# A two-layer pre-activation block on one core: other PReLU paths, statistics in bank ends, another softmax, and a new order

## The chip, the core and the metric

The kernel runs on one core of a Trainium2 chip. The metric is the device time of one execution in microseconds. The core has a matrix engine (TensorE, PE in the profile, its weight loads PEld), a vector engine (VectorE, DVE), an activation engine (ScalarE, ACT), GpSimd (POOL) and SyncE (SP), which here only starts transfers. Matrix products land in PSUM: eight banks of 512 fp32 words in each of 128 partitions. Everything else works on SBUF.

## What is computed

Input x is 16 images of 256 channels, 56 x 56, fp32. Two residual layers follow each other, each on the group-normalised x (32 groups of 8 channels):

```python
def _L0_conv_ref(x, bias, w, cb, move1, alpha, move2, gamma, beta):
    xq = sign(x + bias)
    out = 0
    for i, d in enumerate((1, 3, 5)):               # three dilations, 3x3, 4 channel groups
        y = conv(xq, _bin_weight(w[i]), padding=d, rhs_dilation=d, groups=4)
        y = y + cb[i] - move1[i]
        y = where(y >= 0, y, alpha[i] * y) + move2[i]    # PReLU
        out = out + y
    out = (out - mean_over_channels) * rsqrt(var_over_channels + 1e-5)
    return out * gamma + beta

def _L1_conv_ref(x, ...):                           # 8 heads of 8 channels, 3x3 window
    q, k_in, v_in = 1x1 convolutions of x           # 64 channels each
    k = unfold3x3(k_in) + depthwise3x3(k_in) + biases    # 9 of 8 channels per pixel and head
    v = unfold3x3(v_in) + depthwise3x3(v_in) + biases
    attn = softmax((q * k).sum(channels), over the nine)
    return proj((attn * v).sum(nine))

x = x + _L0_conv_ref(gn(x), ...)
x = x + _L1_conv_ref(gn(x), ...)
```

`_bin_weight` is the sign of the centred weights times their mean absolute value.

## The kernel before

**Tiling.** The 64 channels of a group (NG = 4 groups) lie in partitions twice: the upper half of the image in 64 partitions, the lower half in the other 64. A unit u (two an image) is a strip of 14 rows of each half, cut in two pieces of 7 rows, SN = 392 pixels; a tile of one group and unit is 128 x 2 x 392, written 128x784 in the profile. One pair of PSUM banks holds one such tile, and there are four pairs.

**Stages of an image b.** `signs` loads x by group (xh), takes sums and squares on ScalarE (L643), makes the normalisation's shift in small steps (`group_stats`, `shifts`, 4 columns wide) and writes the signs in bf16 to `sgn` (L667), after which two small transfers copy the halo rows (L679, L680). `conv` multiplies for each unit, group and dilation d: 36 products (9 taps, 4 quadrants of the array) into one pair of banks (L716), and then applies the PReLU. It is split as alpha*y + (1-alpha)*relu(y): for d=0 ScalarE writes alpha*y to the tile ct (L735), for d=1 VectorE adds it to ct (L745), for d=2 ScalarE writes it to a second tile rl (L742); then ScalarE does the relu in place in PSUM (L750), and VectorE adds its share (L755). For d=2 GpSimd adds rl to ct (L761). `channel_norm` squares ct (L799), sums over channels with small products (`lanes_sum`, L769), computes mean and root in steps of 196 columns (L813 to L821), spreads them back over the channels (`lanes_spread`, L783), subtracts the mean (L827), scales (L837), adds to x (L850 on GpSimd) and squares again for the second normalisation (L854). `fold` turns these sums into scaled weights wf (L874) and a bias (L884, L894). `qkv` makes q, k and v (L906, evicted by ScalarE at L924). `scores` makes nine products q*k shifted (L959, mostly on GpSimd), sums them with TensorE (L980, ten terms into one pair of banks) and takes the softmax: transpose, maximum, subtraction, exponentials, sum, reciprocal, product, transpose (L1009 to L1031). The ninth exponential is that of the implied zero-shift term and is kept apart, in the columns behind the scores. `attend` multiplies the weights for ten terms (L1044), VectorE multiplies by v shifted (L1055), GpSimd adds up (L1070), VectorE closes (L1075), and the projection (L1087, L1097) adds to x; four transfers store a unit (L1107).

**The order.** Nothing in this program loops on the chip: every instruction is emitted once, in an order written out by hand or by a program ahead of time. The table `ORDER` gives each operation of each stage a place; image b adds b times `PERIOD`. Keys with ^ hold for the first image, with $ for the last. `Plan.emit` walks the places in order and emits the first operation whose inputs are there and whose buffers are free, so the engines' queues interleave several images' stages: the convolutions of image b+1 stand beside the attention of image b. `ON_VECTOR` names the operations, mostly GpSimd's, that are given to VectorE instead. Each engine takes its own instructions strictly in that order, and semaphores hold an instruction until what it reads is there and what it overwrites has been read. In this framework two instructions that touch the same bank of one PSUM tensor are also ordered.

Buffers are counted: four pairs of banks ("ps"), eight ct, one rl, seven p (products q*k), four m (products with v), four xt (x of a unit).

**Start.** GpSimd clears four sgn tiles and the padded q, k and v tiles (L537); `vectors` (L1115 to L1126) makes per-channel constants on VectorE; six pairs of weight blocks are centred, their signs taken, and transposed by TensorE, and VectorE keeps scales and weights (L1222 to L1224).

Of the kernel before, what the change touches and what calls it, by code (L numbers as in the profile page):

```python
# [34 lines left out]
LANES = 32  # L35
SCALE = (C // NH) ** -0.5
# [36 lines left out]
class Op:  # L73
    def __init__(self, place, emit, bufs):
# [6 lines left out]
PERIOD = 1231  # L81
ORDER = {
    "conv0": (
        -682, -410, -359, -2832, -303, -327, -265, -333, -280, -264, -245, -1566, -289, -213, -969, -970,
        -319, -128, -2067, -24, -3260, -58, -18, -16, -1028, -3936, 5, 17, 18, 101, 198, -321, 208, -3768,
        197, 207, 182, -601, -3937, 20, -15, -19, -199, 30, -146, 111, -2560, 21, -394, -20, -152, -3331,
    ),
    "conv0$": (
        -685, -409, -2692, -2836, -277, -2837, -419, -253, 194, -189, 109, -866, -1791, -207, -131, -440,
        -4781, -30, -3248, 99, -154, -250, -557, -386, -2111, -2366, 32, -462, -149, -2080, 175, -1794,  # L90
        -2185, -2439, 121, 140, -6017, -1732, -220, -9, -641, 100, -155, 112, -1493, 147, -1733, 191, 240,
        149, -865, -2379,
    ),
    "conv0^": (
        -2099, -6338, -223, -5746, -1337, -3215, -66, -5779, -1241, -202, -65, -5786, -1673, 42, -67, -667,
        -358, 124, 92, 358, -3217, 123, 231, 234, -3216, 565, 167, 400, 401, -1668, 228, 318, 504, -54, 229,
        -13, 515, -1726, -288, 227, 402, -115, -71, 40, -72, 517, -1182, 702, -116, -769, -2031, 119,
    ),
    "conv1": (
        160, -122, -123, 185, 199, -740, 209, -834, 265, -287, 150, -2506, -1087, 320, 171, 170, -823, 333,  # L100
        -2428, 361, -1220, 326, -175, 180, -1339, 356, 319, 255, 254, -2493, 355, -1340, 394, -1221, 714,
        746, 632, -113, -2040, 412, -162, -296, -1322, 470, -3611, 514, -1195, 925, -1683, -2369, 905, -1995,
    ),
    "conv1$": (
        56, -644, -645, -1492, 306, -11476, -498, -11477, 418, 239, 237, -3613, 188, 148, 146, 190, -1497,
        248, -878, 152, -867, 292, 151, -2181, -2390, -2392, 192, 98, 66, -864, 773, -432, 813, -1612, 662,
        456, 455, -1613, -818, 419, -28, -29, 44, 774, -431, 816, -434, 953, 968, 284, 678, -660,
    ),
    "conv1^": (
        666, 513, 523, -1198, 726, -697, -757, 826, 776, 581, 725, 830, 871, 682, 522, 601, -2033, 828, 824,  # L110
        695, 832, 829, 724, 578, 835, 715, 711, 612, 609, -2032, 865, 831, 878, 811, 949, 902, 901, 1044,
        1106, 38, 717, 718, 827, 869, 815, 890, -2027, 922, -1136, -964, 940, 959,
    ),
    "first^": (-3247,),
    "fold": (
        1404, -2035, -892, -2087, -3779, -4755, -952, -4221, -7223, -9967, -564, -942, -953, 1414, -949,
        -562, 1455, 407,
    ),
    "fold$": (
        1238, 1089, 753, 927, 1174, 593, 772, 1298, 934, 929, 595, 268, 1484, 297, 648, 1286, 559, -6518,  # L120
    ),
    "fold^": (
        1395, -941, -2847, -582, -784, 793, 792, -861, -863, -1498, -846, 1074, 1037, 696, 1424, -847, 1481,
        1444,
    ),
    "load0": (310,),
    "load0$": (539,),
    "load0^": (744,),
    "load1": (771,),
    "load1$": (614,),  # L130
    "load1^": (-117,),
    "mean0": (
        301, -2124, -1860, -2389, 172,
    ),
    "mean0$": (
        336, 87, 139, -232, -216,
    ),
    "mean0^": (
        785, 930, 214, -4431, 979,
    ),  # L140
    "mean1": (
        719, 911, 1038, -307, 787,
# [218 lines left out]
    "scale0^": (10,),  # L361
    "scale1$": (4,),
    "scale1^": (4,),
    "value0^": (4,),
}


# [1051 lines left out]
```

## Time and profile before

| | us |
|---|---|
| median of 3 runs | 1867.02 |
| lowest and highest | 1861.42, 1869.45 |
| the profiled execution | 1872.31 |
| its span, first to last instruction | 1870.5 |
| its mean granted TensorE clock | 0.979 of full |

| engine | busy us | share of the span |
|---|---|---|
| PE | 1653.7 | 88% |
| VectorE | 1570.8 | 84% |
| GpSimd | 1408.7 | 75% |
| ScalarE | 1314.6 | 70% |

The transfers keep their engines busy for 51.8% of the span. How to read the lines below: a group names the line, engine and operation, then what is written and read with shapes, the count, the busy time and the mean of one, and behind the last bar the idle time of the engine just ahead of these instructions, with what ended it. A line of waits names who waited for whom, for how many us in total, how often, and the longest. A window gives the busy time of PE, PEld, DVE, ACT and POOL in a stretch, each with its count, then the granted clock, the share of the transfer engines and GB/s. Busy times of PE are modelled: an engine that is busy all the time need not run at its full pace.

### The profile page before, as it was taken

The page shows a single profiled execution, that of the slowest core. Times are in us where ns is not written, and L with a number is a line of the kernel's source. Part 1 is how long each engine was busy: PE and PEld are TensorE (multiplying, and loading weights), DVE is VectorE, ACT ScalarE, POOL GpSimd, SP SyncE. Part 2 cuts the span into 40 slices and gives each one's busy share as a digit, 9 for nine tenths or more (in the row PEclk, how much of TensorE's full clock was granted, in tenths as well). Part 3 has the DMA queues.
Part 4 walks back from the last instruction along what each step waited for, and adds up shares of the span by engine and source line. Part 5 has one row for each costly group of instructions (what it writes and reads, how often), then busy time and mean ns, then how long its engine had stood idle before and what let it go on. Part 6 is the DMA issues. An engine that isn't in the chain of part 4 may idle for free.

```text
span 1870.5 us, 62125 instructions
## 1 busy us (share of the span) xinstructions
PE 1653.7 (88%) x27322; PEld 953.1 (51%) x27322; DVE 1570.8 (84%) x2217; ACT 1314.6 (70%) x1861; POOL 1408.7 (75%) x782
## 2 busy tenths in 40 slices
PE   4879899898999989898998989899898989989784
PEld 3546455454545545454554545455454545745341
DVE  8777979979797997979799797979979797997966
ACT  5988778677777867677786777778677787755320
POOL 2147769688686968868696886869688686967865
PEclk9799999999999999999999999999999999999897
DMA  7852655547475554647555464755547467223023
GB/s 178 200 113 43 143 123 122 126 93 155 96 158 111 124 126 92 149 102 155 115 120 124 96 151 101 156 113 124 123 94 150 101 147 172 62 69 74 11 61 69
DMA packets 102094, 217.03 MB, mean 116 GB/s; under 512 B 10816, under 2 KB 84672, under 8 KB 101568
## 3 DMA queue, kind: packets, MB, share of 16 engines
q1 hardware_dynamic: 101824, 213.06, 51.8%
q8 instruction: 214, 3.51, 0.8%
q14 instruction: 56, 0.46, 0.1%
HBM read 156.23 MB, written 51.38 MB: 111 GB/s over the span
## 4 chain that ended last, share of the span: by engine, by line
PE 53%; POOL 18%; DVE 16%; issue 6%; ACT 4%; DMA 1%; SPq 0%; POOLq 0%; DVEq 0%; ACTq 0%
PE banks L716 19%; POOL m L1070 13%; PE banks L906 12%; PE banks L980 9%; DVE m L1055 4%; PE banks L1044 3%; PE banks L769 3%; POOL xt L850 3%; PE banks L1087 2%; ACT banks L750 2%; DVE rl L755 2%; DVE ct L755 2%; POOL p L959 1%; POOL ct L761 1%; DVE m L1075 1%
## 5 line engine op out<-in xcount | busy, mean ns | idle before, releaser
L716 PE MATMUL banks<-sgn,wconv 64*64 64x392 bf16 x13824 | 656.7, 335 | 60.3 <-DVE m L1055 25.8
L716 PEld LDWEIGHTS <-wconv 64*64 64x64 bf16 x13824 | 442.8, 106 | 279.1 <-issue 94.7
L1070 POOL TENSOR_TENSOR m<-m 128x784 f32<-128x784 f32 x255 | 475.3, 1864 | 95.9 <-DVE m L1055 82.2
L959 POOL TENSOR_TENSOR p<-qt,kt 128x784 f32<-128x784 f32 x267 | 468.1, 1789 | 93.2 <-ACT qt L924 88.0
L750 ACT ACTIVATE banks<-banks,cbi,csc 128x784 f32<-128x784 f32 x384 | 370.3, 973 | 95.8 <-DVE ct L745 95.8
L761 POOL TENSOR_TENSOR ct<-ct,rl 128x784 f32<-128x784 f32 x125 | 233.3, 1866 | 252.7 <-DVE ct L755 147.8
L1044 PE MATMUL banks<-at,wv 64*64 64x392 f32 x2560 | 276.1, 510 | 56.5 <-DVE lv L821 22.6
L1055 DVE SCALAR_TENSOR_TENSOR m<-banks,vb,vt 128x784 f32<-128x784 f32 x288 | 289.6, 1022 | 25.4 <-POOL m L1070 17.6
L755 DVE SCALAR_TENSOR_TENSOR ct<-banks,oalpha,ct 128x784 f32<-128x784 f32 x256 | 258.1, 1026 | 17.1 <-ACT banks L750 16.4
L906 PE MATMUL banks<-xt,wf 64*64 64x392 f32 x3072 | 269.0, 491 | 0.0
L850 POOL TENSOR_TENSOR xt<-xt,ct 128x784 f32<-128x784 f32 x124 | 229.2, 1871 | 1.4 <-DVE ct L837 1.3
L980 PE MATMUL banks<-p,wk 64*64 64x392 f32 x2304 | 213.7, 489 | 2.8 <-POOL p L959 2.6
L742 ACT ACTIVATE rl<-banks,asc 128x784 f32<-128x784 f32 x128 | 116.7, 912 | 107.0 <-PE banks L716 103.0
L906 PEld LDWEIGHTS banks<-xt,wf 64*64 64x64 f32 x3072 | 131.2, 133 | 101.2 <-issue 68.3
L643 ACT ACTIVATE xh<-xh 128x1568 f32<-128x1568 f32 x120 | 180.6, 1507 | 0.7
L735 ACT ACTIVATE ct<-banks,mv,asc 128x784 f32<-128x784 f32 x128 | 128.5, 1004 | 73.0 <-PE banks L716 72.8
L755 DVE SCALAR_TENSOR_TENSOR rl<-banks,oalpha,rl 128x784 f32<-128x784 f32 x128 | 131.8, 1030 | 53.6 <-ACT banks L750 48.8
L1044 PEld LDWEIGHTS banks<-at,wv 64*64 64x64 f32 x2560 | 86.8, 134 | 176.3 <-issue 69.2
L745 DVE SCALAR_TENSOR_TENSOR ct<-banks,asc,ct 128x784 f32<-128x784 f32 x128 | 131.0, 1024 | 24.9 <-PE banks L716 21.3
L980 PEld LDWEIGHTS banks<-p,wk 64*64 64x64 f32 x2304 | 93.1, 133 | 93.4 <-issue 76.2
L854 ACT ACTIVATE ct<-xt,pr 128x784 f32<-128x784 f32 x128 | 120.2, 940 | 25.4 <-POOL xt L850 23.0
L1087 PE MATMUL banks<-m,wp 64*64 64x392 f32 x1024 | 106.4, 518 | 32.1 <-DVE m L1075 29.6
(115 smaller groups left out, 1870.6 us busy)
## 6 DMA issues: line engine op xcount, KB each, us to landing
xh<-in_x SPq DMA_DIRECT2D x248, 392.0 KB, 5.7
xt<-in_x SPq DMA_DIRECT2D x128, 392.0 KB, 9.2
out<-xt SPq DMA_DIRECT2D x128, 392.0 KB, 5.9
sgn<-sgn SPq DMA_DIRECT2D x128, 41.2 KB, 7.6
p<-in_w SPq DMA_DIRECT2D x12, 144.0 KB, 3.2
xt<-in_wk_parts SPq DMA_DIRECT2D x1, 1344.0 KB, 8.1
xt<-in_wv_parts SPq DMA_DIRECT2D x1, 1280.0 KB, 9.4
wq<-in_wqkv SPq DMA_DIRECT2D x1, 384.0 KB, 9.7
```

Source lines behind the costliest of these rows:

```text
L643: lambda func=func, col=col: nc.scalar.activation(inside(g) if b == 0 else image(xh), image(xh), func, accum_out=sums[:, col : col + 1]),
L716: nc.tensor.matmul(out=ps[q * GC : (q + 1) * GC, h, 0:SN], lhsT=wconv[h * GC : (h + 1) * GC, g, d, tap, :], rhs=sgn[g][h * GC : (h + 1) * ...
L750: lambda: nc.scalar.activation(n(), n(), AF.Relu, bias=cbi[:, g, s], scale=csc[:, g, s]),
L755: lambda: nc.vector.scalar_tensor_tensor(to.tile, n(), oalpha[:, g, s], to.tile, ALU.mult, ALU.add),
L761: lambda e: e.tensor_tensor(ct.tile, ct.tile, to.tile, ALU.add),
L850: lambda e, g=g: e.tensor_tensor(xt[:, g], xt[:, g], ct[g].tile, ALU.add),
L906: nc.tensor.matmul(out=ps[h * D : (h + 1) * D, q, 0:SN], lhsT=wf[q * GC : (q + 1) * GC, g, j, :], rhs=xt[q * GC : (q + 1) * GC, g, h, :], ...
L959: e.tensor_tensor(p.tile.rearrange("p x (r w) -> p x r w", w=W), _view(qt[:, 0, u * SN :], [(NU * SN + LANES, 2), (W, SR), (1, W)]), shift ...
L980: nc.tensor.matmul(out=ps[q * D : (q + 1) * D, h, 0:n], lhsT=wk[r, j, :], rhs=rhs, start=s == 0, stop=s == 9,)
L1044: nc.tensor.matmul(out=ps[h * D : (h + 1) * D, q, 0:SN], lhsT=wv[q * D : (q + 1) * D, j, :], rhs=at[q * D : (q + 1) * D, h, 0:SN], start=True,
L1055: lambda j=j, m=m, ps=ps: nc.vector.scalar_tensor_tensor(m.tile.rearrange("p x (r w) -> p x r w", w=W), _view(ps[:, 0, :], [(512, 2), (W, ...
L1070: lambda e, m=m, acc=acc: e.tensor_tensor(acc.tile, acc.tile, m.tile, ALU.add),
```

## The change

- **PReLU.** For d=0 and d=2 the relu is the first step and goes to SBUF: ScalarE writes a scaled relu to ct or rl, and VectorE adds alpha*y from PSUM to it, in one pass each. So that one form serves all signs of 1-alpha, the scale's size goes into the relu (rsc, cbi) and its sign (sgd) is brought in later: for d=2 by a ScalarE pass rl to rl, which also adds the bias mv2; for ct in the sums over channels (weights cms) and in the mean's subtraction. d=1 keeps its three passes. There are two rl buffers.
- **Bank ends.** PSUM becomes one tensor of eight banks; the four pairs are views of it. The small statistics and the bias of `fold` get a buffer kind of their own, "few": the columns from 470 of the odd bank of a pair.
- **Small steps.** In `group_stats`, `channel_norm` and `fold` a square, a copy, a clamp and another copy go from VectorE to ScalarE; the signs in the root's last steps are rearranged (ngam in place of gam).
- **Softmax.** The nine exponentials lie side by side in a tile e9 (104 x 9); one sum takes all nine, and the product with the reciprocal is done by GpSimd (by VectorE in the last image).
- **Clearing.** GpSimd clears one sgn tile and VectorE three; q, k and v are cleared by GpSimd behind the constants. Half of the weights' copies go to ScalarE.
- **Places.** PERIOD becomes 1214, and ORDER and ON_VECTOR are new throughout. VectorE takes one product q*k less in each middle image.

```diff
-PERIOD = 1231
+PERIOD = 1214
 ORDER = {
...
 ON_VECTOR = {
-    "conv0$": (12,),
-    "conv1$": (25, 51),
-    "prod0": (5,),
-    "prod0$": (3, 4, 6, 8),
...
+    "prod0$": (2, 4, 6, 8),
+    "prod1$": (3,),
...
+    "soft0$": (8,),
+    "soft1$": (8,),
 }
...
-    kinds = {"ps": (banks, 4)}
+    kinds = {
+        "ps": [banks[:, 2 * i : 2 * i + 2] for i in range(4)],
+        "few": [banks[:, 2 * i + 1 : 2 * i + 2, TAIL:512] for i in range(4)],
+    }
...
-    kind("rl", UNIT, 1)
+    kind("rl", UNIT, 2)
...
-    for t in (*sgn, *qts, *kts, *vts):
-        nc.gpsimd.memset(t, 0.0)
+    for g, t in enumerate(sgn):
+        (nc.vector if g else nc.gpsimd).memset(t, 0.0)
...
-        dve(lambda: nc.vector.tensor_copy(e[:, 0:n], at(0)), [gp], [e])
-        dve(lambda: tt(m2[:, 0:n], at(0), e[:, 0:n], ALU.mult), [gp, e], [m2])
+        act(lambda: nc.scalar.activation(m2[:, 0:n], at(0), AF.Square), [gp], [m2])
+        act(lambda: nc.scalar.copy(e[:, 0:n], at(0)), [gp], [e])
...
+        stt = nc.vector.scalar_tensor_tensor
+        if d == 1:
             dve(
-                lambda: nc.vector.scalar_tensor_tensor(ct.tile, n(), asc[:, g, s], ct.tile, ALU.mult, ALU.add),
+                lambda: stt(ct.tile, n(), asc[:, g, s], ct.tile, ALU.mult, ALU.add),
                 [ps, ("scales", g, d)],
                 [ct],
             )
         act(
-            lambda: nc.scalar.activation(n(), n(), AF.Relu, bias=cbi[:, g, s], scale=csc[:, g, s]),
-            [("scales", g, d)],
-            [ps],
+            lambda: nc.scalar.activation(
+                n() if d == 1 else to.tile, n(), AF.Relu, bias=cbi[:, g, s], scale=rsc[:, g, s]
+            ),
...
+        if d == 1:
+            dve(lambda: stt(ct.tile, n(), oalpha[:, g, s], ct.tile, ALU.mult, ALU.add), [ps], [ct])
+        else:
+            dve(
+                lambda: stt(to.tile, n(), asc[:, g, s], to.tile, ALU.mult, ALU.add),
+                [ps, ("scales", g, d)],
+                [to],
+            )
+        if d == 2:
+            act(
+                lambda: nc.scalar.activation(
+                    to.tile, to.tile, AF.Identity, bias=mv2[:, g : g + 1], scale=sgd[:, g, 2:3]
+                ),
...
-        dve(lambda: tt(t.tile, mean(), ms.tile, ALU.mult), [ps, ms], [t])
+        act(lambda: nc.scalar.activation(t.tile, mean(), AF.Square), [ps], [t])
...
-        dve(lambda: nc.vector.tensor_scalar(mean(), mean(), 0.0, EPS_LN, ALU.max, ALU.add), [], [ps])
+        act(lambda: nc.scalar.activation(mean(), mean(), AF.Relu), [], [ps])
...
-                lambda g=g: nc.vector.tensor_tensor(ct[g].tile, ct[g].tile, mb[:, :, 0:SN], ALU.subtract),
+                lambda g=g: stt(
+                    ct[g].tile, ct[g].tile, sgd[:, g, 0:1], mb[:, :, 0:SN], ALU.mult, ALU.subtract
+                ),
...
+        dve(lambda: nc.vector.tensor_reduce(sm.tile, ex.tile, AX.X, ALU.add), [(ex, 0), (ex, 1)], [sm])
+        dve(lambda: nc.vector.reciprocal(sm.tile, sm.tile), [], [sm])
+        either(
+            lambda e: e.tensor_tensor(
+                ex[:, :, 0:CH], ex[:, :, 0:CH], sm.tile.unsqueeze(2).broadcast_to([P, NBK, CH]), ALU.mult
+            ),
...
+    def clear():
+        for t in (*qts, *kts, *vts):
+            nc.gpsimd.memset(t, 0.0)
+
+    pool(clear, ["identb"], ["border"])
```

Some lines of the changed program that the prediction names: L725 are the convolution's products, L596 those of `group_stats`, L608 to L616 its steps, L671 the last step of `shifts`, L886 the copy of r, L890 and L909 the last vector steps of `fold` and L899 its products, L1044 the softmax's product, L1080 and L1095 the products with v and their sums, L1112 the projection's products.

## The prediction

> **What bounds the kernel now.** I read the busy table first, then the stages, because four engines between 70% and 88% say that no single one bounds the whole.
>
> ```profile
> PE 1653.7 (88%) x27322; PEld 953.1 (51%) x27322; DVE 1570.8 (84%) x2217; ACT 1314.6 (70%) x1861; POOL 1408.7 (75%) x782
> ```
>
> The starts of L871, once an image, are 149.4 us for image 0, then 259.3, 368.1, 476.9 and so on to 1779.2: the steady period is 109 us. The head is 149 us, the tail behind the last fold 91 us. The windows over one period, cut in halves, and the head and tail (busy us of PE, PEld, DVE, ACT, POOL; then clock and DMA):
>
> ```profile
> 0.00:149.40 149.40, 99.44 (x1814) 67.40 (x1818) 117.86 (x217) 114.12 (x147) 45.78 (x28) 0.91 0.70 160
> 694.85:749.38 54.53, 54.53 (x910) 31.11 (x904) 40.61 (x62) 43.94 (x64) 43.13 (x25) 1.00 0.48 108
> 749.38:803.91 54.53, 45.74 (x764) 26.03 (x760) 52.44 (x68) 37.30 (x51) 45.05 (x25) 0.97 0.62 136
> 694.85:803.91 109.06, 100.27 (x1666) 57.15 (x1660) 93.05 (x128) 81.23 (x114) 88.18 (x49) 0.98 0.55 122
> 1779.20:1870.50 91.30, 62.63 (x656) 26.87 (x648) 56.66 (x58) 10.66 (x20) 54.15 (x28) 0.84 0.27 62
> ```
>
> In the first half PE never rests and DVE has 14 us to spare; in the second DVE works 52.4 of 54.5 us and PE idles 9. An image is bounded in turn by PE and by DVE. The waits and the chain of one period say the same, with one warning: in the second half the chain runs for 20 us through POOL's additions (L1070), so POOL is nearly as late there as DVE.
>
> ```profile
> PE banks L716 <- DVE m L1055: 25.8, 26, 1.1
> ...
> PE banks L716 <- DVE ct L837: 15.9, 14, 1.5
> ```
>
> ```profile
> 779.73 1.87 POOL m L1070
> 781.68 1.85 POOL m L1070
> 783.59 1.87 POOL m L1070
> 785.54 1.87 POOL m L1070
> 787.48 1.86 POOL m L1070
> ```
>
> PE at full pace: 72 to 108 convolution products follow each other at 43 ns, the fp32 ones at 84.5 ns (halves of one instruction), the sums and spreads at 42. With the counts of an image that is 864 x 0.043 + 192 x 0.0845 (qkv) + 160 x 0.085 (scores) + 160 x 0.0845 (values) + 64 x 0.0845 (projection) + 192 x 0.042 + about 2.1 of small ones = 96.1 us. To find what comes on top I lay the rows' durations on the built order: DVE's instructions, less the 7% by which its rows overlap (row means sum to 100.6 us an image, busy is 93.1), against PE's. The stretch in which DVE exceeds PE most runs from 46.9 to 85.2 us of PE's work, with 13.8 us of excess. 96.1 + 13.8 = 109.9, and 109.1 is measured. This sum, made of rows, carries the forecast.
>
> **The change, part by part**, per image. The groups of that one period (busy us, mean ns of one), and one line of the timeline of the start:
>
> ```profile
> L1070 POOL TENSOR_TENSOR m<-m 128x784 f32<-128x784 f32 x16 | 29.7, 1856 | 6.1 <-DVE m L1055 5.3
> ...
> L735 ACT ACTIVATE ct<-banks,mv,asc 128x784 f32<-128x784 f32 x8 | 8.0, 1003 | 3.7 <-PE banks L716 3.7
> ...
> L742 ACT ACTIVATE rl<-banks,asc 128x784 f32<-128x784 f32 x8 | 7.3, 912 | 7.4 <-PE banks L716 7.4
> ...
> L1027 DVE TENSOR_TENSOR et<-et,banks 128x832 f32<-128x832 f32 x2 | 2.0, 1012 | 0.0
> ...
> L816 DVE TENSOR_SCALAR banks<-banks 128x196 f32<-128x196 f32 x2 | 0.7, 370 | 0.1
> ...
> L814 DVE TENSOR_TENSOR lv<-banks,lv 128x196 f32<-128x196 f32 x2 | 0.7, 351 | 0.0
> ```
>
> ```profile
> 3.78 6.94 DVE L1118 TENSOR_SCALAR oalpha<-pr 128x12 f32<-128x12 f32 x1
> ```
>
> *PReLU.* For d=0, ACT's L735 goes (8 x 1.003 = 8.0 us); for d=2, L742 goes (8 x 0.912 = 7.3) and an Identity from rl to rl comes. No row has that source; between L799 (0.851, no pointer operands) and L735 (1.003, two) I take 1.0, so 8.0 back. Relu now writes SBUF: 16 x 0.03 = 0.5. ACT loses 7.3 us, but it is not the bound (81 of 109), so that is worth nothing by itself. What counts is that a pair of banks is held for one ACT pass and one DVE pass instead of two and one: about 0.95 us less, 16 times an image. DVE's work here is unchanged, and the second rl buffer frees DVE of waiting for POOL's addition (L755 rl waits only 0.5 us for POOL now: nothing).
>
> *DVE's small steps to ACT.* L814 and L816 (1.44 us), L599 and L600 twice and L871 (0.8) leave DVE; ACT gets some 2.3 us. In the stage of the root two Vector/Scalar handoffs fall away (L817 waited 3.8 us an image for L816).
>
> *Softmax.* The product leaves DVE (2 x 1.012) and the addition of the ninth (2 x 0.266); the sum runs over 936 instead of 832 elements (+0.26). POOL gets two products. No POOL row has runs of 8 or a broadcast; L1070 scaled to 832 elements gives 1.98 us, the high end is double (4.0), the low end L959's rate (1.9). I take 1.98, the nearest row. The Trainium skill, GPSIMD Engine Reference, section 4.1 (Engine selection), speaks against this step: two-input elementwise work belongs on VectorE, GpSimd being about twice slower. The rows agree on the ratio (1.98 against 1.01), and by that rule alone the move costs 32 x 0.97 = 31 us of chain. By the stage it doesn't: in the after order the chain from scores to values has 9 and 14 us of other PE work laid over it, and DVE is the engine that runs out there. I go by the stage.
>
> *Places.* One product of nine that DVE did in 14 middle images goes back to POOL (DVE -1.25, POOL +1.79). The mean's subtraction becomes the three-operand form: 8 x 0.064 = +0.5 on DVE.
>
> Sum for DVE: -2.03 -0.53 -1.44 -0.80 -1.25 +0.26 +0.51 = -5.3, so 93.0 becomes 87.8. POOL: 88.2 + 1.8 + 4.0 = 94.0. ACT: 81.2 -7.3 +2.3 +0.2 = about 76.5. PE: unchanged.
>
> *Bank ends.* The small statistics no longer take a pair of the four; they sit in the last columns of a bank that a pair also uses. In the built order they are then serialised with that pair's other users. The rule behind it is in the Trainium skill, PSUM — Partial Sum Buffer, section "PSUM bank collisions raise a hardware error": two engines must not touch one bank and quadrant at once, at whatever columns. No row of before shows such a wait. The after order has four or five an image in which PE's next product stands directly behind a small step: L725 behind L611 twice, L1112 behind L890 and L909, L899 behind L1080. Each needs two ACT steps of 0.2, two DVE steps of 0.16 and whatever large DVE row is in front (1.0), against 0 to 1.8 us of PE work laid between: 0 to 2.5 us each. Bounds are 0 and 6 us an image (below zero is not excluded: before, the same statistics took one pair of four out of use for ten steps). I take 2.3. Behind the waiting matmul stand convolution and projection products, and for those DVE waits.
>
> *Stretch by stretch.* The same sum on the after order gives 9.4 us as DVE's largest excess (57.2 to 76.6 us of PE's work) in place of 13.8: less work, and more evenly laid. Period 96.1 + 9.4 + 2.3 - 0.8 (by which the sum overshot before) = 107.0, against 109.1: -2.1 us. Over 15 periods -32.
>
> *Head.* POOL's clearing keeps DVE from its first vectors until 10.7 us (the row of L1118). One sgn stays on POOL (2.2 us), three go to DVE as 1254 words each (at POOL's own pace of 1740 words in 1.6 us, 3.5 us), while DVE waits for its first load (3.7 us) anyway; q, k and v (4.6 us of POOL) are cleared behind identb. Some 18 short vector instructions (about 0.1 each) come, and six casts of 0.75 us go to ACT, which is the busiest engine of the head (114 of 149). Net -4 to +4; I take -3. *Tail:* in the last image DVE keeps four products of the first strip, makes one of the second instead of two, and keeps both softmax products; I take 0. SP issues the same 653 transfers; stores and halo copies come in another order, but DMA is at 0.55 of its engines in the period, so nothing.
>
> The profiled execution took 1872.3 us (span 1870.5), 0.3% above the median of 1867.0. 1872.3 - 35 = 1837, on the scale of the median 1832.
>
> **The rivals.**
>
> *A. The statistics' waits are hidden* (they fall where PE waits for DVE anyway). For it: the four lie just behind the stretch in which DVE is late. Then the period is 96.1 + 9.4 - 0.8 = 104.7, -4.4 us: 1867 - 66 - 3 = about 1798.
>
> *B. POOL becomes the bound, and it is slower.* POOL is idle 20.9 us of a period now, 5.5 for q, 10.6 for ct, 5.3 for m. With 94.0 us of work the period is 94.0 plus what remains of that idle time: it decides against the change as soon as more than 15 us remain, and with all of it the period is 115, 1867 + 15 x 6 = about 1955. With products of 4.0 us the limit falls to 11. For it: the chain of the second half already runs through L1070, and in the after order POOL exceeds PE by 12.4 us over one long stretch (15 to 77). Against it: before, POOL exceeds PE by 13.4 in a shorter one, and PE never rested there, so p's seven buffers and the loose places took that up. As a likely size: 18 us idle, 112, 1910.
>
> *C. What is gained is given back*: the stalls are 4 us or more, the period stays within 0.5 us, 1860 to 1874.
>
> **How the numbers follow.** Expected path (1810 to 1855) 0.5; A 0.22; C 0.13; B 0.15. About 0.5% (9 us) is what a measurement of this kernel can tell from no change. The expected path and A are faster, with a little of the expected path's upper end going into "same": faster 0.74, same 0.11, slower 0.15. Range: from A (1795) up into B's lower part (1885).
>
> **What would show it.** Right: L871's successor (L886) every 107 us; DVE about 88 us busy of it and POOL 94; L1044 on POOL at 2.0 us; idle time of PE in front of L725 and L1112 released by L611, L608 and L890, 2 us an image. Wrong: PE idle behind POOL's p, or DVE m waiting for POOL's L1095 by more than the 17.6 us of now; L1044 on POOL at 3 us or more; a period above 109; a head longer than 149 us.

## The result and the profile after

The changed kernel takes 2005.21 us (median of four runs, 2004.01 to 2014.17), against 1867.95 for the kernel before on the same chip: 1.075 times as long, with an interval of [1.0725, 1.0775]. Its profiled execution has a span of 2003.8 us at a mean granted clock of 0.937 (before 1870.5 and 0.979). I had predicted 1832, between 1795 and 1885.

The busy table of the changed kernel:

```profile
PE 1718.5 (86%) x27322; PEld 1011.3 (50%) x27322; DVE 1491.1 (74%) x1998; ACT 1260.8 (63%) x1889; POOL 1474.5 (74%) x829
...
PEclk9888989899899989989999998999899898999987
```

VectorE has 80 us less to do, ScalarE 54 less and GpSimd 66 more, roughly what the change was expected to do. PE, with the same 27322 instructions, is busy for 65 us longer, and it is idle for 285 us (2003.8 - 1718.5) instead of 217. The whole 133 us by which the span grew are these two: 65 of slower products and 68 of idle time.

The 15 steady periods before, then those of the changed kernel with its head and tail, in windows (busy us of PE, PEld, DVE, ACT, POOL, then the clock):

```profile
149.40:1779.20 1629.80, 1491.66 (x24864) 858.86 (x24856) 1396.23 (x1944) 1189.86 (x1694) 1308.82 (x727) 0.99 0.53 115
```

```profile
163.60:1913.10 1749.50, 1555.33 (x24857) 915.27 (x24860) 1328.46 (x1732) 1130.52 (x1699) 1375.39 (x774) 0.95 0.48 107
0.00:163.62 163.62, 101.50 (x1821) 70.55 (x1822) 106.33 (x215) 119.34 (x171) 42.65 (x27) 0.89 0.65 151
1913.11:2003.80 90.69, 61.71 (x648) 25.48 (x640) 56.29 (x52) 10.96 (x21) 56.46 (x29) 0.86 0.24 54
```

The starts of the fold (L886) give a head of 163.6 us (before 149.4), 15 periods of 116.6 (before 108.65, from 149.4 to 1779.2), and a tail of 90.7 (before 91.3). So 120 us were lost in the periods and 14 in the head. In a period VectorE works 88.6 us in the mean (93.1 before), GpSimd 91.7 (87.3) and ScalarE 75.4 (79.3): none of them is the bound, yet the period is longer. PE works 103.7 us of it and idles for 12.9; before it was 99.4 and 9.2.

Groups of one period, from 756.66 to 877.12 us (busy us, mean ns of one, then the idle time in front and what ended it), and behind them VectorE's last PReLU step (L755) in the period of before that the prediction reads:

```profile
L1095 POOL TENSOR_TENSOR m<-m 128x784 f32<-128x784 f32 x16 | 29.8, 1861 | 15.9 <-DVE m L1080 13.5 <-DVE g L614 1.9
...
L766 ACT ACTIVATE rl<-rl,mv,sgd 128x784 f32<-128x784 f32 x8 | 8.3, 1033 | 2.3 <-DVE rl L760 2.3
...
L757 DVE SCALAR_TENSOR_TENSOR ct<-banks,oalpha,ct 128x784 f32<-128x784 f32 x8 | 8.1, 1026 | 5.0 <-ACT banks L750 5.0
L760 DVE SCALAR_TENSOR_TENSOR ct<-banks,asc,ct 128x784 f32<-128x784 f32 x8 | 8.1, 1020 | 10.1 <-ACT ct L750 10.1
...
L1044 POOL TENSOR_TENSOR e<-e,mx 128x832 f32<-128x832 f32 x2 | 3.3, 1659 | 0.0
```

```profile
L755 DVE SCALAR_TENSOR_TENSOR ct<-banks,oalpha,ct 128x784 f32<-128x784 f32 x16 | 16.1, 1026 | 0.3 <-ACT banks L750 0.3
L755 DVE SCALAR_TENSOR_TENSOR rl<-banks,oalpha,rl 128x784 f32<-128x784 f32 x8 | 8.2, 1030 | 4.7 <-ACT banks L750 4.6
```

VectorE, short of time before, now idles 15 us of this period in front of two of its PReLU steps until ScalarE's relu is there (5 before), and GpSimd idles 13.5 us in front of its additions until VectorE's m is there (5.3 before): the time that was freed became waiting.

One-microsecond windows show how PE loses pace. The pause that ends at 868.85 is 3.6 us long; behind it the clock is 0.50 until about 872, and 16 and 18 products are counted in a us in place of 31:

```profile
866.00:867.00 1.00, 0.00 (x0) 0.00 (x0) 1.00 (x2) 0.35 (x3) 0.40 (x1) 1.00 0.00 0
867.00:868.00 1.00, 0.00 (x0) 0.00 (x0) 1.00 (x2) 0.00 (x0) 0.00 (x0) 1.00 0.00 0
868.00:869.00 1.00, 0.15 (x4) 0.14 (x7) 0.70 (x5) 0.00 (x0) 0.72 (x1) 0.93 0.00 0
869.00:870.00 1.00, 1.00 (x16) 0.72 (x15) 0.00 (x0) 0.00 (x0) 1.00 (x1) 0.50 0.00 0
871.00:872.00 1.00, 1.00 (x18) 0.82 (x12) 0.00 (x0) 0.00 (x0) 0.00 (x0) 0.50 0.00 0
873.00:874.00 1.00, 1.00 (x31) 0.82 (x24) 0.91 (x1) 0.05 (x1) 0.00 (x0) 1.00 0.00 0
```

The chain of waits says what PE waited for there (start, duration, engine and line): two large VectorE steps, then the fold's small ones, then 35 products at 90 ns each, where full pace is 43.

```profile
866.19 1.01 DVE ct L760
867.20 0.94 DVE m L1080
868.14 0.08 DVE g L614
...
868.64 0.17 DVE g L890
868.81 0.04 issue
868.85 3.15 PE banks L725 x35
```

These traces hold the clock at 1.00 or 0.50 only, so a mean of 0.937 over 2003.8 us is about 250 us at half pace, and before's 0.979 is about 80. The growth lies in the periods, where the clock is 0.95 after 0.99.

### The profile page after: what moved, and what is told of

Same layout as the page of the kernel before. It is cut to its first block, busy times and chain, and to the rows that moved or that the text cites. A ratio compares the mean times of both kernels' runs of the same rounds, so it can differ in the third digit from the quotient of the medians.

```text
span 2003.8 us, 61947 instructions
## 1 busy us (share of the span) xinstructions
PE 1718.5 (86%) x27322; PEld 1011.3 (50%) x27322; DVE 1491.1 (74%) x1998; ACT 1260.8 (63%) x1889; POOL 1474.5 (74%) x829
## 4 chain that ended last, share of the span: by engine, by line
PE 62%; DVE 19%; ACT 8%; issue 5%; POOL 4%; DMA 2%; SPq 0%; POOLq 0%; DVEq 0%; ACTq 0%
PE banks L725 22%; PE banks L921 12%; PE banks L995 9%; PE banks L1069 6%; DVE m L1080 5%; PE banks L1112 5%; PE banks L782 4%; DVE ct L852 2%; DVE rl L760 2%; POOL m L1095 2%; PE banks L796 1%; DVE ct L840 1%; PE banks L899 1%; ACT ct L750 1%; DVE ct L760 1%
## 5 line engine op out<-in xcount | busy, mean ns | idle before, releaser
L725 PE MATMUL banks<-sgn,wconv 64*64 64x392 bf16 x13824 | 717.2, 352 | 58.3 <-DVE g L890 22.3
L1095 POOL TENSOR_TENSOR m<-m 128x784 f32<-128x784 f32 x256 | 478.0, 1867 | 287.3 <-DVE m L1080 225.4
L725 PEld LDWEIGHTS <-wconv 64*64 64x64 bf16 x13824 | 469.4, 112 | 301.9 <-issue 116.6
L1069 PE MATMUL banks<-at,wv 64*64 64x392 f32 x2560 | 285.8, 511 | 56.8 <-DVE at L1051 28.4
L1080 DVE SCALAR_TENSOR_TENSOR m<-banks,vb,vt 128x784 f32<-128x784 f32 x288 | 287.7, 1026 | 30.4 <-PE banks L1069 27.6
L921 PE MATMUL banks<-xt,wf 64*64 64x392 f32 x3072 | 288.2, 504 | 0.0
L750 ACT ACTIVATE ct<-banks,cbi,rsc 128x784 f32<-128x784 f32 x128 | 127.2, 999 | 94.7 <-PE banks L725 94.4
L757 DVE SCALAR_TENSOR_TENSOR ct<-banks,oalpha,ct 128x784 f32<-128x784 f32 x128 | 130.3, 1027 | 74.1 <-ACT banks L750 73.8
L1069 PEld LDWEIGHTS banks<-at,wv 64*64 64x64 f32 x2560 | 104.9, 135 | 157.5 <-issue 48.6
L750 ACT ACTIVATE banks<-banks,cbi,rsc 128x784 f32<-128x784 f32 x128 | 124.7, 975 | 92.6 <-DVE ct L745 87.9
L750 ACT ACTIVATE rl<-banks,cbi,rsc 128x784 f32<-128x784 f32 x128 | 127.7, 998 | 78.0 <-PE banks L725 59.9
L1122 DVE SCALAR_TENSOR_TENSOR xt<-banks,prb,xt 128x784 f32<-128x784 f32 x128 | 128.9, 1029 | 60.7 <-PE banks L1112 51.6
L766 ACT ACTIVATE rl<-rl,mv,sgd 128x784 f32<-128x784 f32 x128 | 132.4, 1035 | 42.4 <-DVE rl L760 42.4
L760 DVE SCALAR_TENSOR_TENSOR rl<-banks,asc,rl 128x784 f32<-128x784 f32 x128 | 131.8, 1030 | 23.2 <-ACT rl L750 22.3
```

The lines of the kernel that those rows point to most:

```text
L725: nc.tensor.matmul(out=ps[q * GC : (q + 1) * GC, h, 0:SN], lhsT=wconv[h * GC : (h + 1) * GC, g, d, tap, :], rhs=sgn[g][h * GC : (h + 1) * ...
L750: lambda: nc.scalar.activation(n() if d == 1 else to.tile, n(), AF.Relu, bias=cbi[:, g, s], scale=rsc[:, g, s]),
L760: lambda: stt(to.tile, n(), asc[:, g, s], to.tile, ALU.mult, ALU.add),
L921: nc.tensor.matmul(out=ps[h * D : (h + 1) * D, q, 0:SN], lhsT=wf[q * GC : (q + 1) * GC, g, j, :], rhs=xt[q * GC : (q + 1) * GC, g, h, :], ...
L1069: nc.tensor.matmul(out=ps[h * D : (h + 1) * D, q, 0:SN], lhsT=wv[q * D : (q + 1) * D, j, :], rhs=at[q * D : (q + 1) * D, h, 0:SN], start=True,
L1080: lambda j=j, m=m, ps=ps: nc.vector.scalar_tensor_tensor(m.tile.rearrange("p x (r w) -> p x r w", w=W), _view(ps[:, 0, :], [(512, 2), (W, ...
```

## The experiments

Ratios are to the kernel before, run on the same chip (1864 to 1868 us). "Old places" means the table ORDER of before with PERIOD 1231, where an operation that is new takes the place of the one it replaces or follows. In my first theory the bank ends held PE; the rivals were GpSimd's product and the new operations as such.

**The bank ends taken back.**

```diff
-        gp, e, v, m2 = Buf("few"), Buf("g"), Buf("g"), Buf("g")
+        gp, e, v, m2 = Buf("ps"), Buf("g"), Buf("g"), Buf("g")
...
-        bp, bf = Buf("few"), Buf("g")
+        bp, bf = Buf("ps"), Buf("g")
```

> The changed kernel, with the small statistics and the bias of the fold in a pair of banks of their own again (kind ps in place of few); the same places. If the bank ends are the cause (PE, ACT and DVE held by each other's small steps around the fold), the period falls from 116.6 us to 107 to 110 and the time to 1860 to 1900 us; the clock goes back to 0.97. If the new places are the cause whatever the banks, it stays at 1980 or more. If the shortage of pairs costs more than the bank ends did, it is over 2005.

1987.63 us, 1.0632 [1.0614, 1.065], in the range that was given for the new places as the cause. The period is 117.1, so nothing came back there; the head is 145.3 instead of 163.6. PE's waits in the first 165 us show the largest part of it: the statistics' product (L596) stood behind the last user of the pair whose bank it shares. First the changed kernel, then this run:

```profile
PE banks L596 <- DVE rl L760: 13.3, 3, 9.3
```

```profile
PE banks L596 <- DVE rl L760: 1.2, 1, 1.2
```

The bank ends cost 18 us, once, in the head. In the period their waits are there (L890 and L611 below), but with them gone PE waits as long for something else: 261 us in all instead of 271.

**All new operations at the old places**, statistics in pairs of their own.

> All new operations (PReLU, steps on ScalarE, softmax with its product on GpSimd, split clearing) at the old places with PERIOD 1231, statistics in pairs of their own: no bank ends, no new places. If the bank ends or the places are the cause, it is at or under the kernel before: 1820 to 1865 us, from 5 us less of VectorE's work an image. If the operations themselves cost (GpSimd's product late, ScalarE's extra pass rl to rl), it is over 1900.

2042.74 us, 1.0927 [1.0909, 1.0945], period 118.3, clock 0.958: over the 1900 that was given for operations that cost by themselves, and slower than with the new places. The pass rl to rl (L587) has its place directly behind VectorE's step (L581) here, and that is the largest wait:

```profile
ACT rl L587 <- DVE rl L581: 245.1, 122, 4.9
```

ScalarE's pass stands 2.0 us, 122 times, in ScalarE's queue, and all that is queued behind it waits too.

**GpSimd's product back on VectorE**, in all images, at the new places.

```diff
+    "soft0": (8,),
     "soft0$": (8,),
+    "soft0^": (8,),
+    "soft1": (8,),
     "soft1$": (8,),
+    "soft1^": (8,),
```

> The changed kernel with the softmax's product on VectorE in all images. If GpSimd is what makes it slow (rival B of the prediction), the time falls by 3 us an image or more, to under 1955 us. If the bank ends or the places are the cause, it stays within 15 us of 2005.

2132.22 us, 1.1411 [1.1394, 1.1428]: 127 us worse than the changed kernel, outside both figures. The line of the product explains it (count, then the shortest, median and longest in ns):

```profile
L1048 DVE TENSOR_TENSOR e<-e,mx x32: 1025/2357/9115, 223.1 to 2088.4; 128x832 f32<-128x832 f32 x32
```

It is a 1.0 us operation that takes 4.8 us in the mean. The run on the softmax below shows on what it waits. As a test of GpSimd as the bound this run is therefore not clean.

**Only the PSUM tensor with four views**, in the kernel before.

> The kernel before with PSUM as one tensor of eight banks and the four pairs as views of it, nothing else. All theories: no change, 1860 to 1875 us; it is the ground on which the others stand. If the one tensor in itself makes false waits, over 1890.

1867.08 us, 0.9997 [0.9984, 1.001]. How PSUM is allocated costs nothing.

**One group of edits at a time, at the old places.** The new PReLU path alone; the same without its second pass over rl; the softmax alone; the small steps alone:

> The kernel before with the changed PReLU path alone (and the setup that it needs: sign constants, split clearing), at the old places; the second pass over rl (d=2) stands directly behind VectorE's step. The row of the old-places run had 245 us of ScalarE idle in front of that pass, about half of it across other work. Theory 1 (the pass blocks ScalarE's queue while it waits for VectorE, and that is most of the 175 us which the new operations cost at the old places): 1990 to 2045 us. Theory 2 (each of the three groups of edits upsets the old order by about the same): 1900 to 1940. Rival (the shorter path gains as I predicted): 1840 to 1865.

> As the run with the PReLU path alone, with the second pass over rl left out (its bias and sign are then missing from the result; 128 ScalarE instructions of 1.04 us fewer). Theory 1 (ScalarE's queue blocked by the pass): most of the loss goes: 1850 to 1900 us. Theory 2 (the upset order, or the shorter relu chain itself, costs): within 25 us of the run with the pass, 1900 or more.

> The kernel before with the changed softmax alone (nine exponentials side by side, product on GpSimd in all but the last image), at the old places. Theory 1: a small effect of either sign, 1850 to 1890 us (VectorE 2.3 us an image less, GpSimd 4 more, and one hop to GpSimd and back). Theory 2: 1900 to 1940.

> The kernel before with the small steps alone moved from VectorE to ScalarE (statistics' square and copy, the root's square and relu, the fold's copy), at the old places. Theory 1: 1855 to 1885 us (VectorE 2.2 us an image less, two handoffs fewer; ScalarE 2.3 more). Theory 2: 1900 to 1940.

| at the old places | us | ratio | period |
|---|---|---|---|
| PReLU path | 2051.76 | 1.0988 [1.0957, 1.1019] | 119.7 |
| PReLU path without the pass | 1879.25 | 1.007 [1.0045, 1.0095] | 108.5 |
| softmax | 1919.54 | 1.0295 [1.0266, 1.0324] | 112.4 |
| small steps | 1868.55 | 1.002 [1.0009, 1.0031] | 108.65 |

The pass alone costs 172 us, as the first of the two theories stated there has it (with the pass the time is 7 us above that theory's range):

```profile
ACT rl L586 <- DVE rl L580: 236.5, 116, 4.4
```

It takes 1.04 us and ScalarE is busy for 60% of this run, so as work it fits. But it waits for VectorE, and relus for other pairs of banks stand behind it. That is its price at this place, directly behind VectorE's step; no run puts it further back in the old order. Without it the shorter path gains nothing: the period is that of before. The small steps, 2.3 us an image less on VectorE (1570.8 to 1533.4 busy), gain nothing either. The softmax costs 55 us, as the second theory stated there has it; why is not shown. The losses don't add up: 187 us for the PReLU path and 55 for the softmax alone, but 175 for all new operations together.

**The softmax with its product on VectorE**, at the old places:

> The kernel before with the changed softmax and its product on VectorE in all images, at the old places: tells apart the nine exponentials side by side and the product on GpSimd in the 55 us that the two cost together. If the hop to GpSimd is the cost: 1855 to 1875 us. If the form is (strided writes, reduction over nine): 1900 to 1925.

1980.9 us, 1.0622 [1.0607, 1.0638]: 61 us worse than with the product on GpSimd, and neither of my two figures. Groups, and then the timeline around one of these products (start, duration):

```profile
L853 DVE TENSOR_TENSOR e<-e,mx 128x832 f32<-128x832 f32 x32 | 131.3, 4102 | 0.6
```

```profile
1002.24 1.86 POOL L585 TENSOR_TENSOR ct<-ct,rl 128x784 f32<-128x784 f32 x1
1004.06 8.41 POOL L783 TENSOR_TENSOR p<-qt,kt 128x784 f32<-128x784 f32 x5
1005.05 8.31 DVE L853 TENSOR_TENSOR e<-e,mx 128x832 f32<-128x832 f32 x1
```

The product issues at 1005.05 and is not done until about 1013.4, 0.9 us behind the last of GpSimd's five. Both its operands are in SBUF. All 18 of the products over 1.2 us in this trace end 0.9 us behind the end of a GpSimd instruction. The product of before (et with a reciprocal kept in PSUM) took 1.01 us, and so it does on VectorE at the new places, in the run with the old softmax below:

```profile
L856 DVE TENSOR_TENSOR et<-et,banks x32: 1008/1020/1021, 197.9 to 2046.3; 128x832 f32<-128x832 f32 x32
```

The Trainium skill has the rule: SBUF — State Buffer, section "SBUF: two separate sides", says that VectorE with two SBUF inputs and GpSimd take turns under an exclusive lock, held for a whole instruction. The trace agrees that one blocks the other, and shows more: VectorE was kept out over five instructions, not one. The shortest of the new products take 1.01 us too, so their layout costs nothing; what remains is that the reciprocal's move from PSUM to SBUF made GpSimd the cheaper place for this product. No run moves the reciprocal alone.

**The changed kernel without the pass, with the old d=2 path, and with the old softmax** (the last with the statistics in pairs of their own, so it is to be held against 1987.63):

> The changed kernel at its own places with the second pass over rl left out (its bias and sign are missing from the result). Theory 1 (the pass, which makes ScalarE wait for VectorE in order, is the main cost at the new places too, although only 42 us of ScalarE idle time are booked in front of it): period from 116.6 to 110 or less, 1880 to 1925 us. Theory 2 (the new order itself is the cost: its waits of VectorE for ScalarE and of PE for VectorE do not depend on the pass): within 25 us of the changed kernel, 1980 to 2010.

> The changed kernel at its own places, d=2 by the old path (two ScalarE passes over the banks, then VectorE's step), d=0 by the new one: ScalarE has as many passes, but none that waits for VectorE. Theory 1: as without the pass, 1880 to 1940 us (the pair of banks is held one pass longer, so at the upper end). Theory 2: 1980 to 2030.

> The changed kernel at its own places, with the softmax of before (product on VectorE over 832 elements, ninth apart) and the statistics in pairs of their own, so it is to be held against the run with own pairs (1988 us). If the hop to GpSimd costs here what it cost at the old places (55 us, period 3.8 us longer): 1930 to 1950. If VectorE's 2.3 us an image more count as they did when the product was put on VectorE: 2050 to 2110. Theory 1 expects little: 1970 to 2010.

| at the new places | us | ratio | period |
|---|---|---|---|
| without the pass | 2001.92 | 1.0738 [1.0722, 1.0755] | 116.5 |
| d=2 with two passes over the banks | 2054.26 | 1.1019 [1.1001, 1.1037] | 119.4 |
| softmax of before | 2091.44 | 1.1217 [1.1201, 1.1234] | 123.3 |

Here my theory fell. At the new places the pass, which was nearly the whole loss of the PReLU path at the old ones, costs nothing; and each step back to an old operation makes it worse, by 49 us (outside both figures) and 104 (as the second figure had it). The new order was laid for the new operations. What was left to test was the order.

**The old operations at the new places** (PERIOD 1214, two rl buffers, statistics in pairs):

> The operations of before at the places of the changed kernel (period constant 1214, two buffers of rl, which its order needs). It completes the square: old operations at old places 1864, new at old 2043, new at new 2005. If the new order is bad in itself, and the new operations gain within it: 2060 to 2150 us. If the new order is good in itself and the new operations carry the loss: 1850 to 1900.

2185.03 us, 1.1705 [1.1672, 1.1739], period 128.5, above both ranges. That completes the square:

| statistics in pairs | old operations | new operations |
|---|---|---|
| old places | 1864.37 | 2042.74 |
| new places | 2185.03 | 1987.63 |

Within the new order the new operations gain 197 us, within the old one they lose 178; the new order takes 321 from the old operations and gives 55 to the new ones. So neither the operations nor the order is bad in itself: each set does best in the order that was laid for it, but the new pair does not reach before. (The two mixed corners are transplants; nobody laid an order for them.)

Where PE stands is seen in its groups over the 15 periods, by the idle time in front. Before, then the changed kernel: the convolution's products (L716, L725), those with v (L1044, L1069), the fold's (L884, L899) and the statistics' (L587, L596):

```profile
L716 PE MATMUL banks<-sgn,wconv 64*64 64x392 bf16 x12504 | 585.1, 332 | 42.6 <-DVE m L1055 25.8 <-DVE ct L837 13.5 <-DVE et L1027 1.0
L1044 PE MATMUL banks<-at,wv 64*64 64x392 f32 x2400 | 257.3, 505 | 50.3 <-DVE lv L821 22.6 <-DVE rl L755 10.1 <-DVE ct L827 5.6
...
L884 PE MATMUL banks<-g,wf 64*64 64x1 f32 x720 | 22.7, 192 | 0.0
L587 PE MATMUL banks<-g,cst 128*128 128x8 f32 (+1 forms) x118 | 18.7, 266 | 2.7 <-ACT ct L854 2.7
```

```profile
L725 PE MATMUL banks<-sgn,wconv 64*64 64x392 bf16 x12491 | 646.0, 350 | 51.0 <-DVE g L890 22.3 <-DVE g L611 14.7 <-DVE rl L760 7.0
...
L1069 PE MATMUL banks<-at,wv 64*64 64x392 f32 x2400 | 267.5, 506 | 49.4 <-DVE at L1051 23.9 <-DVE m L1080 19.1 <-ACT kt L939 2.5
...
L899 PE MATMUL banks<-g,wf 64*64 64x1 f32 x720 | 31.3, 207 | 29.8 <-ACT wf L889 15.7 <-DVE ct L757 7.1 <-DVE m L1080 6.1
...
L596 PE MATMUL banks<-g,cst 128*128 128x8 f32 (+1 forms) x116 | 19.2, 274 | 51.9 <-DVE ct L760 13.6 <-DVE ct L852 8.5 <-DVE ct L745 7.2
```

The two large groups wait 100 us after 93, nearly as long as before, though for others. What is new is 82 us, after 3, in front of the small products of the fold and the statistics, behind which the rest of PE's queue stands. The run with the statistics in pairs of their own has these lines:

```profile
L725 PE MATMUL banks<-sgn,wconv 64*64 64x392 bf16 x12520 | 630.7, 349 | 69.2 <-DVE ct L760 52.6 <-DVE rl L760 7.8 <-DVE ct L852 3.0
...
L596 PE MATMUL banks<-g,cst 128*128 128x8 f32 (+1 forms) x116 | 17.7, 261 | 35.9 <-DVE m L1080 18.7 <-ACT ct L869 10.8 <-DVE ct L852 5.2
```

There the small products wait 53 us and the two large groups 135, 188 us in all after 182: the bank ends decide which product stands, and not how long PE stands. One releaser shows the orders apart, VectorE's last PReLU step. Before, then the changed kernel with its statistics in pairs, then the old operations at the new places (L528 is the convolution's product, L567 that step):

```profile
PE banks L716 <- DVE ct L755: 7.1, 5, 2.2
```

```profile
PE banks L725 <- DVE ct L760: 54.1, 40, 1.5
...
PE banks L725 <- DVE rl L760: 7.8, 16, 0.6
```

```profile
PE banks L528 <- DVE ct L567: 84.8, 69, 2.4
PE banks L528 <- DVE rl L567: 44.3, 32, 2.4
```

In the old order a convolution seldom met a pair of banks that a PReLU still held. In the new one PE stands directly behind that release, 56 times with the short path and 101 with the long one. The changed kernel itself has, in their place, waits behind the last small steps of the fold and the statistics:

```profile
PE banks L725 <- DVE g L890: 22.3, 10, 3.6
...
PE banks L725 <- DVE g L611: 14.7, 9, 3.7
```

**Is the half clock a cause or a companion?** In the kernel before, at a place where PE never rests, PE is made late in three ways: two pauses of about 2 us an image, the same two filled with products, or one pause twice as long.

```diff
         def products():
+            if u == 1 and g in (0, 2) and d == 1:
+                for h, q in ((0, 0), (1, 1), (0, 1), (1, 0)):
+                    nc.tensor.matmul(
+                        out=ps[q * GC : (q + 1) * GC, h, 0:SN],
...
+                        start=True,
+                        stop=True,
+                    )
+                for _ in range(2):
+                    nc.scalar.copy(ps[:, :, 0:SN], ps[:, :, 0:SN])
             for tap in range(9):
```

That is the run with two pauses. The filled one makes the four products 13 times over and has no copy; the long pause is at g=0 alone and has four copies.

> The kernel before with two pauses of PE an image, put just behind the fold, where PE never rests: in front of two convolutions (second unit, d=1) four spare products, two ScalarE copies of the bank onto itself (about 1.8 us), and only then the products. PE's instructions stay the same but for 8 products an image (0.3 us). Theory C (a pause of about 2 us makes the granted clock fall to a half for at least one window of 3.4 us): besides PE's idle time its busy time grows by 1.7 us or more for a pause: busy 1654 to 1710, clock 0.95 or less, time 1920 to 1970. Rival (a pause costs its length and no more): busy 1660, clock 0.975 or more, 1880 to 1915.

> As the run with pauses, with the pause filled: 52 spare products (about 2.2 us) in front of the same two convolutions and no ScalarE copy, so PE is late by the same 2.2 us but never idle there. Theory C: the clock stays at 0.98, busy grows by 32 times 2.2 = 70 us, and the time by less than that of the pause in spite of it, 1880 to 1915. Rival (a late PE costs the same, paused or filled): within 10 us of the run with pauses.

> As the run with two pauses of 2 us an image, with one pause instead, made of four ScalarE copies (3.6 us and the queue), in front of one convolution an image: PE is late by about the same in all, but rests in one stretch that is longer than a window of the granted clock (3.4 us). Theory C2 (the clock falls only where a window holds little work, and then costs what PE does in the next one): 16 or more windows at half clock more, PE busy from 1671 to 1695 or more, clock 0.965 or less, and the time 1960 to 1990, above the 1953 of the two pauses. Rival (the clock follows, but costs nothing, since PE would wait later anyway): busy grows, time 1935 to 1955.

| | us | ratio | PE busy | clock |
|---|---|---|---|---|
| two pauses | 1952.78 | 1.0463 [1.0424, 1.0502] | 1670.6 | 0.979 |
| two, filled | 1937.85 | 1.038 [1.0341, 1.0419] | 1719.5 | 0.984 |
| one long pause | 1958.05 | 1.0522 [1.0493, 1.0551] | 1683.3 | 0.964 |

PE's waits for the copies, two pauses and then the long one:

```profile
PE banks L727 <- ACT banks L722: 63.4, 32, 3.7
```

```profile
PE banks L727 <- ACT banks L722: 59.4, 16, 5.5
```

Pauses of 2.0 us (63.4 / 32) leave the mean clock where it was; my figure for them was wrong, though the time lies in its range. Pauses of 3.7 us (59.4 / 16) bring it down, and PE's busy time is 13 us longer though it has fewer products; the time, 5 us more, lies between the two figures. The Trainium skill, TensorE: Matmul & The Clock Gate, Part 1, gives 3.4 us as the window after which an idle PE falls to half; these pauses lie on both sides of it and agree.

Such slower products seem to be paid for. Against before, the pauses and PE's longer busy time make 63 + 17 = 80 us in the first run and 59 + 30 = 89 in the third; they cost 88 and 94. In the filled run 66 us of useless products cost 73 (outside both figures). By these sums the kernel before pays for lateness of PE about one to one, whether PE rests, makes spare products or runs at half clock. The step from two pauses to the long one is too small to show it by itself (4 us less of pause, 13 more of busy time, 5 us of time, and the intervals touch), and the copies also put 51 us of work into ScalarE's queue that the filled run does not have. In the changed kernel, then, the half clock follows from PE's rests, and is likely to cost in its turn; no run shows that part there.

**The parts that did not lose**, together at the old places: the short path for d=0, the old one for d=2, the small steps; and the same with the clearing of before.

> A candidate for the best of the parts, at the old places: d=0 by the new short path, d=2 by the old one (no pass that waits for VectorE), the small steps on ScalarE, softmax as before. Together they had no loss in the steady period (108.5 and 108.65 alone): 1850 to 1880 us, 1865 likeliest; the head decides.

> The candidate (short path for d=0, small steps on ScalarE, old places) with the clearing of before: all of it on GpSimd at the start. If the split clearing costs the head what the candidate's trace suggests (first fold at 162.7 against 149.4): head 148 to 153, 1865 to 1870 us. If the other setup (18 sign vectors, casts on ScalarE) does: 1878 to 1884. To beat before by what can be measured it would need 1855 or less, which its period of 108.35 allows only with a head of 143.

1881.41 us, 1.0091 [1.0056, 1.0127], and 1883.53, 1.0099 [1.0085, 1.0113]. The periods are 108.35 and 108.1, 0.3 and 0.5 us below before, and the heads 162.7 and 167.0, which takes it all back. The second time lies in the range that was given for the rest of the setup as the cause; that rest was not taken apart. The split clearing is not what lengthens the head. No version here beats the kernel before.

## Why the prediction was wrong

- **The loads came about as worked out.** VectorE was to fall from 93.0 to 87.8 us an image (88.6 in the mean of the periods), GpSimd to rise to 94.0 (91.7), ScalarE to fall to 76.5 (75.4). The product on GpSimd takes 1.66 us, where I took 1.98; the pass over rl 1.035, where I took 1.0. ScalarE's sum has a slip: with the 0.5 us that is named, the PReLU takes 6.8 us from it and not 7.3.
- **The step that failed is "stretch by stretch".** I took the period as PE's full pace of 96.1 us plus VectorE's largest excess, 9.4 in place of 13.8, so -4.4. That sum holds only what engines have to do, and treats a queue as if its work could start whenever the engine is free. Measured, VectorE's work fell by 4.5 us and the period grew by 8.0: 3.7 of idle time of PE and 4.2 of slower products. Over its full pace PE loses 20.5 us of a period, where the sum left 10.9. The new idle time is in front of the statistics' and the fold's products, 5.4 us a period after 0.2; of these waits the sum names one, L899 behind L1080, inside its 2.3 for the bank ends. VectorE itself has 28 us of a period to spare, 16 before: it waits for ScalarE, and PE waits for it. That the sum met 109.1 for the kernel before (109.9) was no test of it: it does not see how closely a use stands behind the release that it needs, and there the two orders differ.
- **Bank ends.** The 2.3 us an image were there as waits (22.3 + 14.7 us over 16 images is 2.3), but taking them away left the period as it was: another wait stood behind each. As a cost in the period, 0 and not 2.3. I looked mostly at the large products behind the small steps, not at the small products' own waits. I did not cost the bank ends in the head, where they are worth 18 us.
- **The head**, -3 predicted, is +14; with the statistics in pairs it is -4. In the changed order the number was right but for the bank ends; whether for its reasons no run shows. At the old places every run with the changed PReLU and its setup has a head of 157 to 173.
- **The tail**, 0 predicted, is -0.6.
- **PE "unchanged".** Its count is, its pace isn't: 65 us, which I put at nothing.
- **The PReLU step.** "ACT is not the bound, so that is worth nothing by itself" was right for its time, and I looked at ScalarE's pass only as 1.0 us of work. What stands behind it in the queue was not asked; at the old places, directly behind VectorE's step, it is 172 us.
- **The small steps.** The chain of the root changes between ScalarE and VectorE three times, before and after: no handoff fell away there, though ScalarE's wait in it got shorter (53 us before, 16 after).
- **GpSimd.** I weighed the rule of the Trainium skill, GPSIMD Engine Reference, section 4.1, that two-input work belongs on VectorE, and went by the stage. For the new form of the softmax that was right for a reason I did not have: there the product costs 4.1 to 4.8 us on VectorE.
- **The rivals.** Of A the premise held (with the waits gone the period stayed) and the number did not. B is not borne out, though its period with all of GpSimd's idle time, 115, came close to 116.6 by chance: GpSimd idles for 25 us of a period, and with the old softmax, where it has 48 us less to do and VectorE's product takes 1.02 us, the time is longer by 104. Its sign, VectorE's m waiting for GpSimd, went from 17.6 us to 2.3, while GpSimd waits for VectorE 225 us instead of 82 (L1095 adds up, L1080 multiplies):

```profile
POOL m L1095 <- DVE m L1080: 225.4, 63, 11.4
...
DVE m L1080 <- POOL m L1095: 2.3, 4, 0.9
```

 Rival C comes nearest, stalls that give back the gain, but I stopped it at zero. None of the cases had a change of order that costs more than the operations gain, and so the slower side was left 0.15.

What stays open is which places of the new order lose: the waits name the fold's and the statistics' products and the releases of pairs, but no run moved one of these alone. Nor is the half clock's share of the 137 us measured: its products took at most 65 us more of PE's time, and no run changes the clock of the changed kernel alone. What lengthens the head at the old places is open too.

## What to carry to other kernels

When a change replaces a whole order, count for every wait in the new one how much work of the waiting engine lies between the release and the use, small products included: loads that go down buy nothing where one engine stands right behind another. Before an operation goes to an idle engine, ask what is queued behind it there and what it waits for; a 1 us pass, placed directly behind the step it waits for, cost 172 us. And operations and order are to be tried in all four combinations, since each may be laid for the other.

## What the runs showed of the hardware

- VectorE's 128x832 product with both operands in SBUF took 1.01 to 8.33 us beside GpSimd's work in one run and 1.03 to 9.12 in another, the longest ending behind a run of five GpSimd instructions; with one operand in PSUM it took 1.01 to 1.02 us, all 32 times.
- In the kernel before, pauses of PE of 2.0 us left the granted clock at 0.979; pauses of 3.7 us brought it to 0.964. In the changed kernel a pause of 3.6 us was followed by about 3.4 us at 0.50.
